# Two attention layers and two graph convolutions on one core: the pair products' place among the source table's tiles, the length of the first burst of pair scatters, and the queue of one small read

## The chip, the cores and the metric

The kernel runs on one core of a Trainium2 chip. A time is the device time of one execution in microseconds (us); the time before is the median of three runs. The engines are TensorE (PE), VectorE (DVE), ScalarE (ACT) and GpSimd (POOL); SyncE (SP) issues transfers only. DMA transfers are issued from SP, ACT or POOL. In this kernel SP and ACT issue the plain ones, and POOL issues the indirect ones, whose row numbers come from a tile of indices.

## What is computed

The graph has N = 1250 nodes and E = 20000 edges, given by `src`, `dst` (sorted by `dst`) and `edge_type_34` (34 relations); a node has D = 768 features. Cut to what matters:

```python
def gatv2(x, src, dst, Ws, bs, Wd, bd, attn):      # attn: H x 768/H
    fs = (x @ Ws + bs).reshape(-1, H, 768 // H)
    fd = (x @ Wd + bd).reshape(-1, H, 768 // H)
    e = leaky_relu(fs[src] + fd[dst], 0.2)
    logits = einsum('ehd,hd->eh', e, attn)
    ex = exp(logits - segment_max(logits, dst)[dst])
    alpha = ex / segment_sum(ex, dst)[dst]
    return elu(segment_sum(alpha[:, :, None] * fs[src], dst))

h = relu(layernorm(x))
g = gatv2(h, W1s, W1d, attn1)                      # 8 heads
g = layer_norm(g + h) * ln1_w + ln1_b
x = x + layer_norm(gatv2(g, Wos, Wod, attno)) * lno_w + lno_b   # 1 head
h = relu(layernorm(x))
# mean of h[src] for each (relation, dst), times W_rel[relation], summed over the relations
h1 = einsum('rni,rio->no', mean, W_rel) + h @ W_root + b_rgcn
out = segment_sum((h1 @ W_gcn)[src] * dinv[src] * dinv[dst], dst) + (h1 @ W_gcn) * dinv**2 + b_gcn
x = x + out
```

Everything is float32.

## The kernel before

**Ranked nodes.** The nodes are ordered by falling degree and cut into ten tiles of 128. Tile k has a fixed number of slots per node, `CAPS = (33, 22, 20, 18, 17, 16, 15, 14, 13, 11)`, 179 in all. Row s of tile k is 128 edges, one for each of its nodes. `fast_front` finds the ranks and writes, with ten indirect scatters on POOL (L938), each node's record into the table `f_rank_d` in DRAM: its number, its degree and its 33 edge slots, 35 int32 (140 bytes). One read (L949) then brings all 1280 records into `rk`, 128 partitions by ten records. From `rk` DVE makes `f_perm` (L950) and `f_permg` (the node numbers), the degrees and the source numbers `rec`; ACT makes `dinv` from the degrees (L1375).

**The source table.** `sources(j)` (L833 to L846) makes 128 rows of the first attention's table f_fs_d: on PE twelve matmuls for the 768 columns and the 8 head sums (L839) and two for the bias (L840), each of which is two instructions in the trace, then two ACT copies into `o_s` (L843, L844), and a write by SP (L845). It is called for tile 0 ahead of the read of the ranked nodes, and for tiles 1 to 9 at the end of `fast_front`. Tile 9 has 98 rows.

**The pair lists.** `pairs()` (L960 to L1088) works out for every edge the place of a record in the table `r_pair_d`, by which the third layer later collects the edges of each (relation, destination) pair. DVE counts the edges of each relation per node and makes three masks; for each mask PE makes a running count over the nodes (L991, L993) and a total (L1000), and ACT copies them out (`pre` L997, `tot` L1002). DVE works on these (from L1007 and L1023), then picks for each of the ten tiles an edge's place out of a table of 34 relations (`pick` L1045, `pl` L1046), and writes `place` (L1088). A small product `fl_ps` (L1083) tells whether the limits on the lists hold.

**The first attention.** `attention` runs over the 179 rows, in chunks of at most 20 rows of one tile (tile 0 in 16 and 17). For each row, `front(c, i)` gathers 128 rows of the source table on POOL (L1164, called with `fs`) into one of 24 buffers, and DVE takes the maximum with the negated destination row (`z`, L1228), multiplies by the attention vector (L1233) and sums by head (L1234). `softmax` (L1240 on) takes a chunk's maximum and has ACT's exp (L1252) and DVE's `den` (L1254). `back(c, i)` scales each row's eight heads on ACT (L1286) and adds it up on PE (L1288), after which the buffer can be gathered into again.

The destination rows of tile k come from `negated1` (L1403 to L1415): a gather of `h` on POOL (L1164), its transposes on PE and copies on ACT (L1123 to L1125), 24 matmul instructions with `f_w1d` (L1135), and `nfd` on DVE (L1414). Program order has this for a tile one or two ahead.

**The pair scatters.** 179 scatters on POOL (L1168, into `r_pair_d`) write the records; each has the `place` of one row of edges as its index. `list_edges(row, slots)` (L1383) adds `slots` to a balance and puts as many scatters as it holds behind the given gather. The first call gives 30, behind the 24th gather of the first attention (L1218); later ones give 0.85 for each gather; 7 and 40 come behind the row scatters of the eighth and ninth tile in `finish1` (L1437), and 4 behind the last gather. What is left of 179 goes by then.

**The order of the work.** The engines run their instructions in order. The program's scheduler settles the order of each engine's instructions from the program's order, the dependences and a plan of times; `issue_after` and manual dependences without a semaphore tell it what is to stand ahead of what. In the kernel before POOL has this order around the change: the rank scatters (L938), the gather of h for tile 0, 24 gathers of source rows, the gathers of h for tiles 1 and 2, 30 pair scatters, then gathers and scatters in turn. PE has the source tiles 1 to 9, the count products, the transposes of tile 0's h, `fl_ps`, the product for tile 0's destination rows, the same for tile 1, and the aggregations. On ACT the copies of tile 1's transposed h stand ahead of the first exp. The weights of the second attention, `wos` and `wod` (SP, L1176) and five rows (ACT, L1181) are loaded into room that `pairs()` gives back.

Of the kernel before, what the change touches and what calls it, by code (L numbers as in the profile page):

```python
# [18 lines left out]
P = 128  # L19
# [6 lines left out]
WIN = 64  # L26

PT = 4
DT = 5
PX = 3  # L30
P2, P3, OC = 160, 32, 6
PC = PT + 3

# [593 lines left out]
def fast_front(ctx, tc, f, x, src, dst, edge_type, W1s, b1s, W1d, b1d, attn1, attno, W_rel):  # L627


    nc = tc.nc  # L630
# [3 lines left out]
    R = W_rel.shape[0]  # L634
# [3 lines left out]
    NT = len(CAPS)  # L638
    NP = NT * P
# [22 lines left out]
    rank_d = dram.tile([NP, 2 + S0], I32, name="f_rank_d")  # L662
# [15 lines left out]
    f.h2_d = dram.tile([NP + P, D], F32, name="r_h2_d")  # L678
    f.ZERO = NP + (PT + 1) * P
    f.h1_d = dram.tile([f.ZERO + 1, D], F32, name="r_h1_d")  # L680
# [3 lines left out]
    with ExitStack() as front:  # L684
# [21 lines left out]
        for j in range(NT):  # L706
            n = min(P, N - j * P)
            t = xp.tile([P, D], F32, name=f"x{j}", tag=f"x{j}")
            nc.sync.dma_start(t[:n], x[j * P:j * P + n, :])
            xs.append(t)  # L710
        QW = HW + H // 2
        w1s = wp.tile([P, KC, 2, QW], F32, name="w1s")
# [72 lines left out]
        hT = early.tile([P, KC, NP], F32, name="hT")  # L785
        for j in range(NT):
            n = min(P, N - j * P)
            row = xs[j]
            sc, sh = norm_scale(nc, small, f, row, n)
            nc.scalar.activation(row[:n], row[:n], AF.Relu, bias=sh[:n], scale=sc[:n])  # L790
            nc.sync.dma_start(f.h0_d[j * P:j * P + n, :], row[:n])
            to_columns(nc, ps_t, f, hT, j, row, n, both=True)
        xstack.close()

# [4 lines left out]
        fill = prep.tile([P, COLS, 3], I32, name="fill")  # L799
# [3 lines left out]
        nc.vector.tensor_scalar(fill[:, :, 0], ones_c, lane, None, op0=ALU.mult)  # L803
        for t in range(PT + 1):
            cols = fill[:, :R * PC, 1].rearrange("p (r c) -> p r c", c=PC)[:, :, t] if t < PT else fill[:, R * PC:, 1]
            n = R if t < PT else PX
            nc.vector.tensor_scalar(cols, ones_c[:, :n], lane, float(t * P), op0=ALU.mult, op1=ALU.add)
        nc.vector.memset(fill[:, :R * PC, 1].rearrange("p (r c) -> p r c", c=PC)[:, :, PT:], 0)
        nc.sync.dma_start(f.pair_d.rearrange("(p c) f -> p c f", p=P), fill)
        zero = prep.tile([P, D], F32, name="zero")  # L810
        nc.vector.memset(zero, 0.0)
        nc.sync.dma_start(f.h2_d[NP:, :], zero)
        for t in range(PT + 1):
            nc.sync.dma_start(f.h1_d[NP + t * P:NP + (t + 1) * P, :], zero)
        nc.sync.dma_start(f.h1_d[f.ZERO:, :], zero[:1])


        quarter = SLOPE / (1.0 - SLOPE)
# [14 lines left out]
        def sources(j):  # L833

            n = min(P, N - j * P)
            ps = ps_m.tile([P, 2, 512], F32, name="ps", tag="ag")
            for half in range(2):
                for k in range(KC):
                    nc.tensor.matmul(ps[:n, half, :QW], hT[:, k, j * P:j * P + n], w1s[:, k, half], start=(k == 0), stop=False)  # L839
                last = nc.tensor.matmul(ps[:n, half, :QW], ones_row[:, :n], bias1[:, half], start=False, stop=True)  # L840
            o = work.tile([P, H, HD + 1], F32, name="o_s", tag="o_s", bufs=3)
            ov = o.rearrange("p (a h) d -> p a h d", a=2)
            nc.scalar.copy(ov[:n, :, :, :HD], ps[:n, :, :HW].rearrange("p a (h d) -> p a h d", d=HD))  # L843
            nc.scalar.copy(ov[:n, :, :, HD], ps[:n, :, HW:QW])  # L844
            nc.sync.dma_start(f.fs_d[j * P:j * P + n, :], o[:n].rearrange("p h e -> p (h e)"))  # L845
            return last  # L846

        gotf = prep.tile([P, NT, RW], F32, name="gotf")
        nc.vector.tensor_copy(gotf, got)
# [49 lines left out]
        for g in range(2):  # L899
            wide = ps_m.tile([P, 2, 512], F32, name="wide", tag="ag").rearrange("p a b -> p (a b)")  # L900
            for lo, hi in ((0, 512), (512, N // 2)):
                at = slice(g * (N // 2) + lo, g * (N // 2) + hi)
                nc.tensor.matmul(wide[:, lo:hi], ones16[:EP], flat2[:, at], start=True, stop=False)
                last = nc.tensor.matmul(wide[:, lo:hi], big16[:EP], flat[:, at], start=False, stop=True)
# [39 lines left out]
        with tc.issue_after(last_keys.ins):  # L944
            sources(0)


        rk = prep.tile([P, NT, 2 + S0], I32, name="rk")
        nc.sync.dma_start(rk, rank_d.rearrange("(k p) f -> p k f", p=P))  # L949
        nc.vector.tensor_copy(f.perm, rk[:, :, 0])  # L950
        nc.vector.tensor_scalar(f.permg, rk[:, :, 0], float(N - 1), None, op0=ALU.min)
        nc.vector.tensor_copy(f.degf, rk[:, :, 1])
# [7 lines left out]
        def pairs():  # L960
            tri = pp.tile([P, P], BF16, name="tri")
            nc.vector.tensor_scalar(tri, iota_f, iota_p, 1.0, op0=ALU.subtract, op1=ALU.is_gt)
            ones_b = pp.tile([P, P], BF16, name="ones_b")
# [21 lines left out]
            mask = pp.tile([P, 3, NT, R], BF16, name="mask")  # L985
            pre, tot = [], []
            for i in range(3):
                nc.vector.tensor_scalar(mask[:, i], cnt, float(i + 1), None, op0=ALU.is_ge)
                pps = ps_t.tile([P, 2, 512], F32, name="pp", tag="mm2")
                ppv = pps[:, 0, :NT * R].rearrange("p (k r) -> p k r", r=R)  # L990
                nc.tensor.matmul(ppv, tri, mask[:, i], start=True, stop=False)  # L991
                for k in range(NT - 1):
                    nc.tensor.matmul(ppv[:, k + 1:, :], ones_b,  # L993
                                     mask[:, i, k:k + 1, :].to_broadcast([P, NT - 1 - k, R]),
                                     start=False, stop=(k == NT - 2))
                a = pp.tile([P, NT, R], F32, name=f"pre{i}")
                nc.scalar.copy(a, ppv)  # L997
                tp = pps[:, 1, :]
                for k in range(NT):
                    nc.tensor.matmul(tp[:, :R], ones_b, mask[:, i, k, :], start=(k == 0), stop=(k == NT - 1))  # L1000
                b = pp.tile([P, R], F32, name=f"tot{i}")
                nc.scalar.copy(b, tp[:, :R])  # L1002
                pre.append(a)
                tot.append(b)

            for i in range(2):
                nc.vector.tensor_sub(pre[i], pre[i], pre[i + 1])  # L1007
# [35 lines left out]
            for k, S in enumerate(CAPS):  # L1043
                t = pp.tile([P, R, S0], F32, name="pick", tag="pick")
# [7 lines left out]
            later = pp.tile([P, NT, S0], F32, name="later")  # L1052
# [34 lines left out]
            nc.vector.tensor_scalar(pad, pad, none, None, op0=ALU.add)  # L1087
            nc.vector.scalar_tensor_tensor(f.place, pad, float(P * COLS), pl, op0=ALU.mult, op1=ALU.add)  # L1088

        for j in range(1, NT):  # L1090
            sources(j)
        rows_only.close()
        ranking.close()
        pp = front.enter_context(tc.tile_pool(name="f_pp", bufs=1, side="right"))
# [50 lines left out]
def fast_rest(ctx, tc, f, x, src, dst, edge_type, W1s, b1s, W1d, b1d, attn1, ln1_w, ln1_b,  # L1145
              Wos, bos, Wod, bod, attno, lno_w, lno_b, W_rel, W_root, b_rgcn, W_gcn, b_gcn, out):
    nc = tc.nc
    N, D, NT, NP, KC, HW, S0 = f.N, f.D, f.NT, f.NP, f.KC, f.HW, f.S0
    R = W_rel.shape[0]
# [39 lines left out]
    def attention(H, table, negated, attn_e, first, loads, finish, rate, rest, give_back=lambda: None):  # L1189
# [21 lines left out]
        def front(c, i):  # L1211

            t, s = c.t, c.first + i
            fs = pool.tile([P, RW], F32, name="fs", tag="fs", bufs=ring)
            row = gather(fs[:, :W], table[:, :], f.rec[:, t.k, s, 0:1])
            fs = fs[:, :W].rearrange("p (h e) -> p h e", h=H)
            if t.k == 0 and s == ring - 1:
                list_edges(row, 30)  # L1218
            elif t.k or s >= ring:
                list_edges(row, rate)  # L1220
            if t.k == NT - 1 and s == t.S - 1:
                list_edges(row, rest)
                f.last_row = row
            if t.lg is None:
                lg = pool.tile([P, S0 * f.H], F32, name="lg", tag="lg", bufs=2)
                t.lg = lg[:, :S0 * H].rearrange("p (s h) -> p s h", h=H)
            z = rows_tile("z", 2)
            nc.vector.tensor_tensor(z, fs, t.nfd, op=ALU.max)  # L1228
            if H == 1:
                nc.vector.scalar_tensor_tensor(z[:, 0, :], z[:, 0, :], 1.0, attn_e[:, 0, :], op0=ALU.mult,  # L1230
                                               op1=ALU.mult, accum_out=t.lg[:, s, :])
            else:
                nc.vector.tensor_mul(z, z, attn_e)  # L1233
                nc.vector.tensor_reduce(t.lg[:, s, :], z, axis=AX.X, op=ALU.add)  # L1234
            c.rows.append(fs)
# [81 lines left out]
        for k, S in enumerate(CAPS):  # L1317
            parts = -(-S // CHUNK)
            assert parts <= 2
            for i in range(parts):  # L1320
                c = Tile()
                c.k, c.first, c.n, c.rows = k, S * i // parts, S * (i + 1) // parts - S * i // parts, []
                chunks.append(c)
        tiles = {}
# [58 lines left out]
    def list_edges(row, slots):  # L1383

        due[0] += slots
        while due[0] >= 1.0:
            due[0] -= 1.0
            if edges:
                k, s = edges.pop(0)
                with tc.issue_after(row.ins):  # L1390
                    scatter(pair_d[:, :], f.rec[:, k, s, :], f.place[:, k, s:s + 1], "pair",
                            bounds_check=P * COLS - 1, oob_is_err=False)
# [207 lines left out]
    ahead = first_half(0)  # L1600
# [14 lines left out]
    nc.vector.tensor_copy(own_f, f.perm)  # L1615
    adj = rq.tile([P, NT, DT * P], F32, name="adj")
    srcz = rq.tile([P, NT, S0], I32, name="srcz")
# [19 lines left out]
    wgcn = rq.tile([P, KC, D], F32, name="wgcn")  # L1637
    slots_left = [(k, s) for k in range(DT) for s in range(CAPS[k])]

    slots_each = len(slots_left) / (2 * R)  # L1640
    with three:
        adjacency_slots(ahead)
        for i in range(len(jobs)):
# [3 lines left out]
            ahead = first_half(i + 1) if i + 1 < len(jobs) else None  # L1647
# [9 lines left out]
    with ExitStack() as four:  # L1657
# [32 lines left out]
        def by_rows(k):  # L1690

            acc = gp.tile([P, D], F32, name="acc", tag="acc", bufs=NT - DT)
            gather(acc, h1_d[:, :], f.permg[:, k:k + 1])
# [19 lines left out]
        neighbours(0, 4 * P)  # L1713
        neighbours(4 * P, DT * P)
        for k in range(NT - 1, DT - 1, -1):
            by_rows(k)
            if NT - 1 - k < DT:
                last(NT - 1 - k)
# [48 lines left out]
```

## Time and profile before

| | us |
|---|---|
| median of three runs | 2768.38 |
| lowest and highest run | 2763.95, 2773.92 |
| the profiled execution | 2772.99 |
| its span | 2771.2 |
| busy PE / DVE / POOL / ACT in the span | 2355.7 / 1560.9 / 1549.0 / 852.4 |

The mean granted TensorE clock was 0.930. By stretches of the span (busy us of each engine; POOL's busy time leaves out about 0.3 us between two of its transfers):

| stretch | what runs | PE | DVE | ACT | POOL |
|---|---|---|---|---|---|
| 112 to 175 | source tiles 1 to 9, count products begin | 62.15 | 32.83 | 5.88 | 0.00 |
| 175 to 257 | pair places, first rows of the first attention | 26.77 | 80.01 | 4.76 | 62.73 |
| 257 to 292 | first aggregation, pair scatters | 29.77 | 15.79 | 34.09 | 28.44 |
| 292 to 400 | first attention, steady | 63.09 | 98.20 | 73.18 | 88.07 |

A line of a timeline reads: start in the span and duration in us, engine, line of the kernel, operation, the tile written and the tiles read, shapes, how many instructions are folded into the line, and in brackets how long the engine had been idle before it and what ended the wait. L1164 and L1168 are two helpers, for all gathers and all scatters, so those are told apart by the names of their tiles.

### The profile page before, as it was taken

What the parts mean: (1) busy time and instruction counts of PE and PEld (TensorE: products, weight loads), DVE (VectorE), ACT (ScalarE), POOL (GpSimd) and SP (SyncE); (2) the same over time, 40 slices, a digit from 0 to 9 for tenths busy, and PEclk for the clock granted to TensorE, in tenths of its full rate; (3) what the DMA queues carried; (4) which work ended last, traced back from release to release, by engine and by line L of the source; (5) the groups of instructions that cost most, each with busy time, mean ns of one, the idle gap of its engine ahead of it and who ended that gap; (6) DMA issues with size and microseconds to landing.
All of it is one profiled execution on the core that took longest, in us unless ns stands there. A gap on an engine that the chain in (4) does not pass through costs nothing. (4 is left out here: it accounts for less than half of the span.)

```text
span 2771.2 us, 24164 instructions
## 1 busy us (share of the span) xinstructions
PE 2355.7 (85%) x7759; PEld 1365.4 (49%) x7759; DVE 1560.9 (56%) x2360; ACT 852.4 (31%) x2308; POOL 1549.0 (56%) x1113
## 2 busy tenths in 40 slices
PE   3874484889998467889899999999999999999687
PEld 2431142445545234444456666666666666666254
DVE  7659779999996799999563222222232222210262
ACT  3003592778773122333312112211221212212010
POOL 3137787777872675778375544444444454431471
PEclk7986797999999788999999999999999999999899
DMA  7134453444540775677477777777777777766783
GB/s 248 41 128 146 115 147 95 127 129 131 154 123 29 246 234 170 202 214 216 160 241 194 200 189 187 189 197 197 192 194 187 185 191 197 174 165 152 217 264 117
DMA packets 136419, 476.82 MB, mean 172 GB/s; under 512 B 26323, under 2 KB 28396, under 8 KB 136285
## 3 DMA queue, kind: packets, MB, share of 16 engines
q0 software_dynamic: 83872, 334.60, 46.4%
q1 hardware_dynamic: 47755, 134.03, 13.6%
q10 hardware_dynamic: 4658, 6.57, 0.7%
q8 instruction: 64, 1.05, 0.1%
q14 instruction: 70, 0.57, 0.1%
HBM read 385.90 MB, written 89.32 MB: 171 GB/s over the span
## 5 line engine op out<-in xcount | busy, mean ns | idle before, releaser
L1135 PE MATMUL ps<-wrel,mT 128*128 128x384 f32 x3336 | 1099.1, 486 | 1.1 <-DMA wrel<-in_L_gnn_W_rel_dram 1.1
L1135 PEld LDWEIGHTS ps<-wrel,mT 128*128 128x128 f32 x3336 | 623.0, 190 | 407.1 <-DMA wrel<-in_L_gnn_W_rel_dram 1.0
L1164 POOL DMA_INDIRECT g<-r_h_d,lists x241 | 341.9, 1419 | 516.9 <-DVE g L1565 290.7
L1288 PE MATMUL ag<-fs,identf 128*128 128x384 f32 x716 | 286.9, 532 | 152.4 <-ACT fs L1286 142.0
L1565 DVE TENSOR_TENSOR g<-g,g 128x768 f32<-128x768 f32 x68 | 64.6, 950 | 612.5 <-DMA g<-r_h_d,lists 512.6
L1228 DVE TENSOR_TENSOR z<-fs,nfd 128x776 f32<-128x776 f32 (+1 forms) x358 | 348.5, 990 | 60.0 <-DMA fs<-f_fs_d,rec 37.2
L1286 ACT ACTIVATE fs<-fs,lg 128x96 f32<-128x96 f32 x1376 | 370.0, 363 | 0.3
L1278 PE MATMUL ag<-fs,dg 128*128 128x384 f32 x716 | 251.7, 512 | 81.0 <-ACT dg L1276 81.0
L1168 POOL DMA_INDIRECT r_pair_d<-rec,place x179 | 259.5, 1450 | 59.9 <-issue 46.7
L1164 POOL DMA_INDIRECT fs<-r_fs_d,rec x179 | 244.0, 1363 | 80.7 <-issue 33.4
L1592 POOL DMA_INDIRECT r_h_d<-y,lists x139 | 223.9, 1611 | 110.2 <-ACT y L1591 52.3
L1164 POOL DMA_INDIRECT fs<-f_fs_d,rec x179 | 236.7, 1323 | 77.0 <-issue 50.2
L1288 PEld LDWEIGHTS ag<-fs,identf 128*128 128x128 f32 x716 | 132.4, 200 | 294.0 <-ACT fs L1286 236.5
L1278 PEld LDWEIGHTS ag<-fs,dg 128*128 128x128 f32 x716 | 141.3, 200 | 188.0 <-ACT dg L1276 88.1
L1591 ACT ACTIVATE y<-ps,lists 128x768 f32<-128x768 f32 x71 | 64.0, 901 | 479.8 <-PE ps L1135 479.8
L1591 ACT ACTIVATE y<-ps,rcnt 128x768 f32<-128x768 f32 x68 | 61.3, 901 | 454.6 <-PE ps L1135 454.6
L1230 DVE SCALAR_TENSOR_TENSOR z<-z,attn_o 128x769 f32<-128x769 f32 x179 | 174.4, 993 | 0.0
L1697 DVE TENSOR_TENSOR acc<-acc,nb 128x768 f32<-128x768 f32 x69 | 66.2, 959 | 187.1 <-DMA nb<-r_h_d,srcz 186.3
L1233 DVE TENSOR_TENSOR z<-z,attn 128x776 f32<-128x776 f32 x179 | 168.5, 955 | 0.1
L1234 DVE TENSOR_REDUCE lg<-z 128x8 f32<-128x776 f32 x179 | 168.0, 950 | 0.1
L1627 DVE SCALAR_TENSOR_TENSOR arow<-node,from_f,arow 128x1250 f16<-128x1250 f16 x110 | 166.2, 1511 | 1.7
L1123 PEld LDWEIGHTS pt<-identf,g 128*128 128x128 f32 x834 | 99.8, 141 | 47.5 <-issue 24.5
(282 smaller groups left out, 2322.0 us busy)
## 6 DMA issues: line engine op xcount, KB each, us to landing
wrel<-in_L_gnn_W_rel_dram SPq DMA_DIRECT2D x37, 2304.0 KB
g<-r_h_d,lists POOLq DMA_INDIRECT x241, 4.8
r_nfd_d<-fd SPq DMA_DIRECT2D x10, 384.0 KB
nfd<-r_nfd_d SPq DMA_DIRECT2D x10, 384.0 KB
r_x_d<-xb SPq DMA_DIRECT2D x10, 384.0 KB
x1r<-r_x_d SPq DMA_DIRECT2D x10, 384.0 KB
f_fs_d<-o_s SPq DMA_DIRECT2D x9, 388.0 KB
x<-in_x_dram SPq DMA_DIRECT2D x9, 384.0 KB
```

Source lines behind the costliest of these rows:

```text
L1135: last = nc.tensor.matmul(ps[:n, half, :f.HW], hT[:, k, j * P:j * P + n], w[:, k, cols], start=(k == 0), stop=(k == f.KC - 1 and not bias))
L1164: return nc.gpsimd.indirect_dma_start(out=to, out_offset=None, in_=table, in_offset=bass.IndirectOffsetOnAxis(ap=idx, axis=0))
L1168: s = nc.gpsimd.indirect_dma_start(out=table, out_offset=bass.IndirectOffsetOnAxis(ap=idx, axis=0), in_=rows, in_offset=None, **kw)
L1228: nc.vector.tensor_tensor(z, fs, t.nfd, op=ALU.max)
L1230: nc.vector.scalar_tensor_tensor(z[:, 0, :], z[:, 0, :], 1.0, attn_e[:, 0, :], op0=ALU.mult, op1=ALU.mult, accum_out=t.lg[:, s, :])
L1233: nc.vector.tensor_mul(z, z, attn_e)
L1234: nc.vector.tensor_reduce(t.lg[:, s, :], z, axis=AX.X, op=ALU.add)
L1278: nc.tensor.matmul(c.ps[:, half, :HW], dg, fs[:, 0, half * HW:(half + 1) * HW], start=begin, stop=end)
L1286: nc.scalar.activation(fs[:, h, :HD], fs[:, h, :HD], AF.Copy, scale=t.lg[:, s, h:h + 1])
L1288: nc.tensor.matmul(c.ps[:, half, :HW].rearrange("p (h d) -> p h d", d=HD), f.identf, fs[:, half * H // 2:(half + 1) * H // 2, :HD], start= ...
L1592: s = nc.gpsimd.indirect_dma_start(out=h1_d[:, :], out_offset=bass.IndirectOffsetOnAxis(ap=j.node, axis=0), in_=y, in_offset=None, compute ...
L1627: nc.vector.scalar_tensor_tensor(a, node16, from_f[:, k, s:s + 1], a, op0=ALU.is_equal, op1=ALU.add)
```

## The change

The ranked nodes are read by POOL instead of SP. The tenth source tile's twelve matmuls and its last bias product get a dependence, without a semaphore, on the last of the count products, so that they stand behind them on PE. The first burst of pair scatters is 24 instead of 30. The zero writes of four tables are told to stand behind the last write of `h0`.

```diff
+TL = 9
...
-            nc.sync.dma_start(f.h0_d[j * P:j * P + n, :], row[:n])
+            h0_write = nc.sync.dma_start(f.h0_d[j * P:j * P + n, :], row[:n])
...
-        nc.sync.dma_start(f.pair_d.rearrange("(p c) f -> p c f", p=P), fill)
+        with tc.issue_after(h0_write.ins):
+            nc.sync.dma_start(f.pair_d.rearrange("(p c) f -> p c f", p=P), fill)
...
         def sources(j):
 
             n = min(P, N - j * P)
+            mine = []
...
-                    nc.tensor.matmul(ps[:n, half, :QW], hT[:, k, j * P:j * P + n], w1s[:, k, half], start=(k == 0), stop=False)
+                    mine.append(nc.tensor.matmul(ps[:n, half, :QW], hT[:, k, j * P:j * P + n], w1s[:, k, half],
+                                                 start=(k == 0), stop=False))
                 last = nc.tensor.matmul(ps[:n, half, :QW], ones_row[:, :n], bias1[:, half], start=False, stop=True)
+            mine.append(last)
...
-            return last
+            return mine
...
-        nc.sync.dma_start(rk, rank_d.rearrange("(k p) f -> p k f", p=P))
+        nc.gpsimd.dma_start(rk, rank_d.rearrange("(k p) f -> p k f", p=P))
...
-                    nc.tensor.matmul(tp[:, :R], ones_b, mask[:, i, k, :], start=(k == 0), stop=(k == NT - 1))
+                    ahead = nc.tensor.matmul(tp[:, :R], ones_b, mask[:, i, k, :], start=(k == 0), stop=(k == NT - 1))
...
+            for i in behind:
+                tc.add_manual_dep(i.ins, ahead.ins.name, mybir.DependencyInfo(
+                    mybir.DependencyClass.NoSync, mybir.DependencyReason.DATA), reason="the table's last tiles later")
...
-        for j in range(1, NT):
+        for j in range(1, TL):
             sources(j)
+        behind = []
+        for j in range(TL, NT):
+            behind += sources(j)
...
-                list_edges(row, 30)
+                list_edges(row, 24)
```

The writes of zeros to `h2_d` and `h1_d` get `issue_after` like that of `pair_d`; on SP they stood behind the `h0` writes already.

How the order of the instructions moves, engine by engine: on PE the three passes of count products stand between the ninth and the tenth source tile, and ACT's copies follow. On SP the read of the ranked nodes is gone (it stood behind two writes of `o_s` and ahead of eight). On POOL that read stands behind the rank scatters, ahead of tile 0's gather of h; then come 24 gathers, 24 pair scatters, the gathers of h for tiles 1 and 2, and gathers and scatters in turn; before the tenth tile's row scatter there are 13 pair scatters instead of 7. On DVE all of the picks up to `place` stand ahead of the first `nfd` and the first `z`, where the first seven or so rows' z instructions stood between them.

More of the change, by code (lines that the diff above doesn't have):

```diff
@@ L808, in fast_front @@
         nc.vector.memset(fill[:, :R * PC, 1].rearrange("p (r c) -> p r c", c=PC)[:, :, PT:], 0)
-        nc.sync.dma_start(f.pair_d.rearrange("(p c) f -> p c f", p=P), fill)
+        with tc.issue_after(h0_write.ins):
+            nc.sync.dma_start(f.pair_d.rearrange("(p c) f -> p c f", p=P), fill)
         zero = prep.tile([P, D], F32, name="zero")
         nc.vector.memset(zero, 0.0)
-        nc.sync.dma_start(f.h2_d[NP:, :], zero)
+        with tc.issue_after(h0_write.ins):
+            nc.sync.dma_start(f.h2_d[NP:, :], zero)
         for t in range(PT + 1):
-            nc.sync.dma_start(f.h1_d[NP + t * P:NP + (t + 1) * P, :], zero)
-        nc.sync.dma_start(f.h1_d[f.ZERO:, :], zero[:1])
+            with tc.issue_after(h0_write.ins):
+                nc.sync.dma_start(f.h1_d[NP + t * P:NP + (t + 1) * P, :], zero)
+        with tc.issue_after(h0_write.ins):
+            nc.sync.dma_start(f.h1_d[f.ZERO:, :], zero[:1])
         quarter = SLOPE / (1.0 - SLOPE)
```

## Prediction

> **What bounds the kernel now.** I read the times first. The profiled execution took 2772.99 us and its span is 2771.2 us. The median of the three runs is 2768.38 us, 4.6 us less. I work on the clock of the profiled span and put the shift that comes out onto the median. About 0.3%, 8.3 us, is what a measurement of this kernel can tell from no change.
>
> Second I read the page's busy shares: PE 85%, DVE 56%, POOL 56%. They are averages over stages. The change sits between 106 us and 290 us, so I next read each engine's timeline there. This is the source table's last tile and what follows it, from the timeline of PE:
>
> ```profile
> 162.56 4.15 PE L839 MATMUL ps<-w1s,hT 128*98 128x388 f32 x12
> ...
> 172.37 0.32 PE L991 MATMUL pp<-mask,tri 128*128 128x340 bf16 x1
> ...
> 179.06 0.44 PE L1000 MATMUL pp<-mask,ones_b 128*128 128x34 bf16 x10 [0.53 <-ACT pre L997]
> ```
>
> The tenth tile holds PE from 162.56 to 172.4 (9.8 us), and then the three passes of count products run to 179.5 (7.1 us). DVE waits for the products, from its timeline:
>
> ```profile
> 174.60 0.18 DVE L1023 TENSOR_SCALAR more<-tot 128x34 f32<-128x34 f32 x1 [29.31 <-ACT tot L1002]
> ...
> 187.04 1.33 DVE L1045 TENSOR_TENSOR pick<-same,pdf 128x1122 f32<-128x1122 f16 x1
> ...
> 195.67 0.96 DVE L1414 SCALAR_TENSOR_TENSOR nfd<-ps,bias 128x768 f32<-128x768 f32 x1 [0.29 <-PE ps L1135]
> ...
> 225.69 0.49 DVE L1088 SCALAR_TENSOR_TENSOR place<-pad,pl 128x330 int32<-128x330 f32 x1
> ...
> 291.02 0.97 DVE L1228 TENSOR_TENSOR z<-fs,nfd 128x776 f32<-128x776 f32 x1 [19.21 <-DMA fs<-f_fs_d,rec]
> ```
>
> DVE is idle for 29.3 us ahead of 174.60, then without a gap to 271.8, and then idle for 19.2 us until the 25th source row is there. That row is late because of POOL, from its timeline:
>
> ```profile
> 177.15 1.16 POOL L1164 DMA_INDIRECT h<-f_h_d,f_permg  x1 [71.91 <-DVE hit L1062]
> ...
> 217.42 1.49 POOL L1164 DMA_INDIRECT h<-f_h_d,f_permg  x1 [0.30 <-issue]
> ...
> 226.47 2.37 POOL L1168 DMA_INDIRECT r_pair_d<-rec,place  x1 [5.54 <-DVE place L1088]
> ...
> 272.96 0.97 POOL L1168 DMA_INDIRECT r_pair_d<-rec,place  x1 [0.30 <-issue]
> ...
> 287.00 0.99 POOL L1164 DMA_INDIRECT fs<-f_fs_d,rec  x1 [0.30 <-PE ag L1288]
> ```
>
> The 30 pair scatters hold POOL from 226.47 to 286.7. Under an unbroken stream of z rows one scatter passes every 2.62 us, the length of one row's three DVE instructions; with DVE idle one takes 0.97 plus 0.30 (1.28 us). The 25th gather stands behind them. After 292 POOL sets the pace: in 292 to 400 it has 65 instructions, 88.07 us busy, and 65 gaps of 0.30 fill 107.6 of the 108 us. So the number to follow is **when the 25th gather issues, now 287.00**: a shift of it goes through to the end.
>
> **The change part by part.**
>
> *Ranked nodes by GpSimd's queue.* SP now issues the read at 106.89 (0.37 us) and DVE uses it at 109.68, 2.79 us later. PE's next tile waits for it too, since ACT, in its order, has dinv (which needs the ranked nodes) ahead of the table's copies: PE stands idle 9.86 us until 111.15. So a delay d here moves all that follows. Nothing is queued on POOL behind it until the h gather at 177, and the SP writes that stood behind it lose nothing. The trace has no POOL transfer of this shape (1280 runs of 140 bytes). Bounds: d is 0 if it costs what SP's does. The upper end takes the shortest 128-row gather, 0.94 us, as if all of it were by row: 7.4 ns for each of 1280 rows, 9.4 us, d = +9. Between: the shortest 32-row gathers (g at L1164) take 0.86 us and the shortest 128-row one 0.94, so about 0.8 ns a row over a fixed 0.84: 1.9 us for 1280 rows, and with some 2.4 us of landing 4.3 us, d = **+1.5**. I take that, as it separates the fixed part.
>
> The Trainium skill, "DMA: Bandwidth & Descriptors", Specifications, speaks against this step: first byte at about 1 us by the gpsimd path, about 0.6 us by the sync path. By that alone d would be an estimated +0.4; no run here shows such a read on POOL yet.
>
> *Products ahead of the tenth tile.* On PE the products move 9.8 us earlier (162.6 + d), the tenth tile 7.1 us later (to 179.5 + d). ACT's copies go along. DVE starts its chain at 164.8 and the first pick 12.4 us later at 177.2. Today 39.06 us lie between the first pick and the end of the place at 226.1; 19 z instructions at 0.875 (16.6), one nfd (0.87) and 0.3 of idle are in it, so the picks alone take 21.3 us. The changed program has all of them ahead of nfd and the z's: **place at 198.5 + d instead of 226.1**.
>
> *What is late next.* The h gather of tile 0 waits for every write of the table to land, the tenth tile's too: now 4.7 us after PE ends it (172.4 to 177.15), so at 184.2 + d, 7.1 us later. From gather to nfd is 18.5 us now, of which 1.3 are PE waiting for the flag's product, gone afterwards: nfd at 201.5 + d, against 195.67. DVE is idle for 3 us there, which costs nothing yet, since DVE has 19.2 us of waiting to give.
>
> *The order on POOL.* First burst 24, not 30. But the scatters now stand behind the 24th gather and **ahead of the h gathers of tiles 1 and 2**; today those go first. ACT, in order, has the copies of tile 1's columns ahead of the first exp, and PE has that tile's transposes and product ahead of the first aggregation. So tile 1's h gather, which now issues at 217.42 with time to spare, gets onto the path: from its issue 4.1 us to the transposes (as at 177.15 to 181.26), 1.5 for them, 9.7 for the product, 1.1 for row 0's aggregation: **25th gather at h + 16.4**. Break-even is h at 270.6.
>
> When does h issue (without d)? POOL starts the gathers at 185.7. Today's 24 take 38.5 us, 1.6 each. By 202.4, when z starts, 10.4 have gone. The other 13.6 go under z rows: at 1.6 they end at 224.2, at 2.62 at 238.0. From nfd DVE has 0.87, then 55 z instructions at 0.875 and 1.2 of small ones until it must wait for the exp, at 251; until then scatters pass at 2.62, that is 10.2 of them or 5. The other 13.8 or 19 pass beside an idle DVE at 1.28: h at 268.7 or 275.3. Middle 272, with d 273.5; 25th gather at 289.9: **+2.9 us**. DVE agrees: exp some 8.2 us after h (transposes, copies, table), then den and 12.6 us of rows left, 25th z at h + 21.6 = 295.1 against 291.02, +4.1, of which a few gathers that have gone ahead by then give some back. ACT starts its 128 scalings (34.1 us) some 25 us later, but its next exp (322.93) has 31.8 us of slack now.
>
> *Weights.* The wos and wod loads (2304 KB each) wait for the place and come at 198.5 instead of 226, beside the gathers. The windows there show 243 to 294 GB/s; the rows are used at one per 2.62 us and have 16 us of lead, so I cost it at nothing. Without that cover POOL's gathers get later; that is in the 2.62 bound.
>
> *The six scatters less* go to the burst between the last two row scatters of the first attention, 7 to 13. Those 7 run from 882.59 to 892.2, 1.37 each; 13 end near 900, and the next row scatter waits for DVE until 905.36: hidden, 5 us to spare. The new issue orders of the zero writes move nothing.
>
> Which price holds for POOL under z's? At 226 to 254 the pitch is 2.62; at 292 to 400, with DVE busy 98.2 of 108 us, it is 1.65. The Trainium skill, "SBUF — State Buffer", Who interferes with whom, says that a DVE instruction with two SBUF inputs shuts out a GpSimd one that reads SBUF, and that a reduce doesn't. The first stretch agrees, the second only in part. By the rule each costs a z row: h at 275.3, an estimate of +6.2 in all.
>
> **The rivals.**
>
> *About the same (forecast):* +2.9, 2768.4 + 2.9 = **2771**. Speaks for it: both ends of the POOL sum lie within 5 us of break-even.
>
> *Faster:* POOL passes its DMAs at 1.65 under z's, as at 292 to 400. Gathers end at 224, 16.2 scatters pass by 251, the other 7.8 take 10: h at 261, 25th gather 277.4 + d. With d = 0, -9.6, **2759**. Against it: one scatter per 2.62 us in the very stretch of z's that this one repeats. At 1.28 throughout DVE would set the 25th z near 267 and the time near 2745, which no stretch under z's shows.
>
> *Slower, the other side:* the h gather of tile 1 behind 24 scatters becomes the bound. If gathers go at 2.62 and the remaining 19 scatters at their mean of 1.45 + 0.30 even while DVE waits, h is at 284.3, with d 285.8, 25th gather 302.2: +15, **2784**. It decides from h later than 270.6. For it: nothing else can release ACT and PE. Against: beside an idle DVE each takes 1.28.
>
> *The read costs by row on POOL:* d = +9 instead of 1.5, **2779**.
>
> *It does nothing:* the picks come early but nothing waits for them, and h lands at break-even: 2768.
>
> **How the numbers follow.** Forecast and nothing together 0.56; faster 0.17; slower through the h gather 0.19; slower through the read 0.08. The range goes from a little under the faster case to a little short of the slow one: 2757 to 2782.
>
> **What would show it.** The first product on PE near 164, the place near 200, the h gather of tile 0 near 186, nfd near 203. The read's use on DVE 4.3 us after its issue. On POOL, 24 scatters between the 24th gather and tile 1's h, that one near 273; DVE's idle time ahead of den, about 30 us from 252, in place of the 19.2 at 291; 25th gather near 290. I am wrong if h issues before 262 or after 279, if the read takes over 8 us, or if ACT's late scalings hold up row 25 to 32.

## The result and the profile after

The changed kernel takes 2780.74 us (median of 7 runs, 2776.43 to 2791.15); the kernel before, with four more runs, 2773.01. The ratio is 1.0045, with a 95% interval of 1.0029 to 1.0061: slower by 8 to 17 us. The profiled execution took 2778.47 us, with a span of 2776.7.

Around the change it went nearly as the forecast had it. The timeline of PE after:

```profile
162.95 0.32 PE L999 MATMUL pp<-mask,tri 128*128 128x340 bf16 x1
...
168.90 0.40 PE L1008 MATMUL pp<-mask,ones_b 128*128 128x34 bf16 x10 [0.53 <-ACT pre L1005]
169.15 4.13 PE L845 MATMUL ps<-w1s,hT 128*98 128x388 f32 x12
```

The products start 9.4 us earlier, and the tenth tile follows them. The timeline of DVE after:

```profile
110.50 0.17 DVE L958 COPY f_perm<-rk 128x10 int32<-128x10 int32 x1 [20.37 <-DMA rk<-f_rank_d]
...
176.35 1.33 DVE L1056 TENSOR_TENSOR pick<-same,pdf 128x1122 f32<-128x1122 f16 x1
...
199.90 0.50 DVE L1099 SCALAR_TENSOR_TENSOR place<-pad,pl 128x330 int32<-128x330 f32 x1
200.32 0.95 DVE L1428 SCALAR_TENSOR_TENSOR nfd<-ps,bias 128x768 f32<-128x768 f32 x1
...
278.58 0.38 DVE L1268 TENSOR_REDUCE den<-lg 128x8 f32<-128x128 f32 x1 [28.36 <-ACT lg L1266]
```

The place is ready at 200.4 instead of 226.2, and the 19.2 us that DVE waited for the 25th row are gone. In their place DVE waits 28.4 us, from 250.2 on, for ACT's first exp, ahead of den. The timeline of POOL after:

```profile
106.90 1.03 POOL L957 DMA_DIRECT2D rk<-f_rank_d  x1 [1.91 <-DMA f_rank_d<-rec,rank_i]
183.80 1.03 POOL L1178 DMA_INDIRECT h<-f_h_d,f_permg  x1 [75.88 <-DVE pick L1056]
...
228.25 3.77 POOL L1182 DMA_INDIRECT r_pair_d<-rec,place  x1 [0.30 <-issue]
...
270.92 0.99 POOL L1178 DMA_INDIRECT h<-f_h_d,f_permg  x1 [0.30 <-issue]
272.22 0.96 POOL L1178 DMA_INDIRECT h<-f_h_d,f_permg  x1 [0.30 <-issue]
287.13 2.27 POOL L1178 DMA_INDIRECT fs<-f_fs_d,rec  x1 [13.94 <-PE ag L1302]
```

The scatters come right behind the gathers (228.25), tile 1's h gather stands behind all 24 at 270.92, and POOL waits 13.94 us for the first aggregation. The 25th gather issues at 287.13, against 287.00 before. So up to here the change has neither won nor lost, and the question is what costs the 8 to 17 us after that.

### The profile page after: what moved, and what is told of

Its sections match the earlier page's. It is cut to its first block, busy times and chain, and to the rows that moved or that the text cites. A ratio compares the mean times of both kernels' runs of the same rounds, so it can differ in the third digit from the quotient of the medians.

```text
span 2776.7 us, 24171 instructions
## 1 busy us (share of the span) xinstructions
PE 2347.5 (85%) x7759; PEld 1364.6 (49%) x7759; DVE 1562.6 (56%) x2360; ACT 852.0 (31%) x2308; POOL 1536.9 (55%) x1114
## 5 line engine op out<-in xcount | busy, mean ns | idle before, releaser
L1302 PE MATMUL ag<-fs,identf 128*128 128x384 f32 x716 | 279.1, 522 | 111.6 <-ACT fs L1300 101.3
L1178 POOL DMA_INDIRECT fs<-f_fs_d,rec x179 | 243.6, 1361 | 94.0 <-issue 49.7
L1182 POOL DMA_INDIRECT r_pair_d<-rec,place x179 | 253.2, 1414 | 56.4 <-issue 46.0
L1711 DVE TENSOR_TENSOR acc<-acc,nb 128x768 f32<-128x768 f32 x69 | 66.2, 959 | 184.2 <-DMA nb<-r_h_d,srcz 183.5
L1137 PE MATMUL pt<-identf,h 128*128 128x128 f32 x120 | 22.1, 334 | 123.0 <-DMA h<-f_h_d,f_permg 82.5
```

The costliest lines, as they stand in the source:

```text
L1178: return nc.gpsimd.indirect_dma_start(out=to, out_offset=None, in_=table, in_offset=bass.IndirectOffsetOnAxis(ap=idx, axis=0))
L1182: s = nc.gpsimd.indirect_dma_start(out=table, out_offset=bass.IndirectOffsetOnAxis(ap=idx, axis=0), in_=rows, in_offset=None, **kw)
L1302: nc.tensor.matmul(c.ps[:, half, :HW].rearrange("p (h d) -> p h d", d=HD), f.identf, fs[:, half * H // 2:(half + 1) * H // 2, :HD], start= ...
```

## The experiments

Each run is compared with the kernel before on the same chip, in five rounds. In the table the shift of the 25th gather is against 287.00, from one profile each; the time in us is the ratio less one, times 2770.

| run | 25th gather | ratio (95%) | us |
|---|---|---|---|
| **read by SP or ACT, or another small read on POOL** | | | |
| products, burst 30 | +6.0 | 1.0031 (1.0019 to 1.0044) | +8.6 |
| products, burst 24 | -1.1 | 1.0017 (1.0007 to 1.0026) | +4.7 |
| burst 24 | -6.2 | 0.9971 (0.9957 to 0.9986) | -8.0 |
| burst 24, read by ACT | -6.0 | 0.9968 (0.9955 to 0.9980) | -8.9 |
| burst 24, five memsets on POOL | -7.5 | 0.9975 (0.9964 to 0.9986) | -6.9 |
| burst 24, and one record read on POOL | -6.8 | 0.9978 (0.9965 to 0.9991) | -6.1 |
| burst 24, and 640 records read on POOL | -5.2 | 0.9977 (0.9964 to 0.9989) | -6.4 |
| products, burst 24, h gather first | -7.9 | 0.9971 (0.9959 to 0.9983) | -8.0 |
| products, burst 20, h gather first | -10.6 | 0.9956 (0.9941 to 0.9971) | -12.2 |
| burst 20 | -14.4 | 0.9952 (0.9935 to 0.9968) | -13.3 |
| **1280 records read on POOL** | | | |
| the read alone (burst 30) | +2.4 | 1.0015 (1.0003 to 1.0027) | +4.2 |
| the whole change | +0.1 | 1.0045 (1.0029 to 1.0061) | +12.5 |
| the whole change, h gather first | -8.8 | 1.0008 (0.9995 to 1.0022) | +2.2 |
| burst 24 and the read | -7.9 | 1.0007 (0.9996 to 1.0018) | +1.9 |
| burst 24, second read that nobody uses | -6.9 | 1.0001 (0.9990 to 1.0013) | +0.3 |
| burst 24, the read, sixteen memsets | -8.4 | 1.0001 (0.9990 to 1.0012) | +0.3 |
| burst 25 and the read | -5.7 | 0.9987 (0.9976 to 0.9997) | -3.6 |
| burst 20 and the read | -13.0 | 0.9942 (0.9926 to 0.9957) | -16.1 |

**The parts alone.** The read:

```diff
-        nc.sync.dma_start(rk, rank_d.rearrange("(k p) f -> p k f", p=P))
+        nc.gpsimd.dma_start(rk, rank_d.rearrange("(k p) f -> p k f", p=P))
```

> The kernel before with one edit: the ranked nodes are read by GpSimd's queue. The profile after shows 3.60 us from issue to use against 2.79, so by the theory of the forecast (what comes later at the 25th gather comes later at the end) this is +0.8 us, no change to be seen. By the rival that the read carries the loss (its queue, or what it does to the transfers behind it), this alone is +8 us or more.

Measured +4.2 us (0.8 to 7.5): more than the 0.8, less than the 8. Undecided by itself. The burst:

```diff
-                list_edges(row, 30)
+                list_edges(row, 24)
```

> The kernel before with one edit: a first burst of 24 pair scatters instead of 30. By the theory that the 25th gather sets the end, POOL has 6 scatters of 1.28 us less ahead of it: the 25th gather at 279.3 instead of 287.0 and a time 6 to 8 us lower. By the rival that the six scatters cost as much where they go (the burst behind the ninth tile's row scatter, or between gathers), the time is as before or higher by up to 8 us.

Measured -8.0 us, the 25th gather at 280.77. DVE's wait for the 25th row has shrunk by 7.7 us, which is six scatters of 1.28; timeline of DVE with the burst of 24 alone:

```profile
284.70 0.97 DVE L1228 TENSOR_TENSOR z<-fs,nfd 128x776 f32<-128x776 f32 x1 [11.47 <-DMA fs<-f_fs_d,rec]
```

So the burst is a gain by itself, and the scatters that it drops cost nothing where they go. The products alone, which is the changed kernel with

```diff
-        nc.gpsimd.dma_start(rk, rank_d.rearrange("(k p) f -> p k f", p=P))
+        nc.sync.dma_start(rk, rank_d.rearrange("(k p) f -> p k f", p=P))
...
-                list_edges(row, 24)
+                list_edges(row, 30)
```

> The changed kernel with the read on SP's queue again and the burst of 30: the move of the count products alone. By the theory that the 25th gather sets the end, the h gather of tile 1 stands behind six scatters more, 270.9 - 0.8 + 6 x 1.28 = 277.8, and the 25th gather comes at 294: +7 us against before, and 7 us over the run with the burst of 24. By the rival that the loss of the change arises behind the 25th gather, from ACT's scalings that start 22 us late, this run loses about as much as the one with the burst of 24 and the two lie within 3 us.

and with the first of these two edits only:

> The changed kernel with the read on SP's queue again; the count products ahead of the tenth tile and the burst of 24 stay. By the theory of the forecast it lies 0.8 us under the changed kernel, and by its 25th gather at 286.3 no more than 1 us from before. By the rival that the read carries the loss it is as before or faster. By the rival that the loss arises behind the 25th gather from ACT's late scalings it is 8 to 12 us over before, as the changed kernel is.

The products alone are +8.6 us, with tile 1's h gather at 276.30 and the 25th gather at 293.02, within 2 us of what was expected. With the burst of 24 it is +4.7 us where the 25th gather promised -1.1: an excess of 5.8, for which its interval leaves 3 to 8. The whole change lies another 7.8 us higher, and all it has more is the read.

**Is it the h gather's place?** Tile 1 is begun two rows earlier, so that its h gather is ahead of the 24th gather:

```diff
-                if i == now.n // 2:
+                if i == (6 if j == 0 and H > 1 else now.n // 2):
                     begin(j + 2)
```

> The changed kernel with tile 1's h gather ahead of the 24th gather (the tile is begun two rows earlier), so that exp and the aggregations don't wait for the 24 scatters. The theory that the h gather's place behind the scatters costs time: exp near 250, DVE streams on to 266, scatters at one per 2.62 us until then and at 1.28 after, the 25th gather near 280 instead of 287 and a time 6 to 8 us under the changed kernel. The rival that the loss lies elsewhere (the read, or ACT's and PE's backlog behind the 25th gather for another reason): within 2 us of the changed kernel.

> As the run before it, with the ranked nodes read by SP's queue again: the products ahead of the tenth tile, the burst of 24 and tile 1's h gather ahead of it. If the read costs what its own span shows, it lies 0.8 us under that run; if the read costs what the runs of the first group showed, 2 to 8 us under it. By the 25th gather's place it lies 6 to 8 us under before, about where the burst of 24 alone lies: the products' move is then worth nothing even without its side effect.

Both are 10 to 13 us under the same kernels without the edit, and their 25th gathers 7 to 9 us earlier: the h gather behind the scatters is what made the products' move lose. With SP's read the excess of 5.8 is gone as well (gather -7.9, time -8.0). But the two differ by 0.37%, some 10 us, in nothing but the read. And -8.0 us is just what the burst alone gives, so the products' move itself has gained nothing.

**The read on another base, and how far the burst goes.** The read's edit and the burst of 24 on the kernel before; then the kernel before with `list_edges(row, 20)`:

> The kernel before with a burst of 24 and the read on GpSimd's queue; products and h gathers stay. By the read's own span (3.6 us from issue to use, not 2.79) it is 0.8 us over the run with the burst of 24 alone, 2763. By the rival that the read costs more than its span, it is 4 us or more over it, 2766 to 2770.

> The kernel before with a burst of 20 alone. By the theory of the 25th gather, ten scatters less are 12.8 us less ahead of it: it issues near 274 and DVE's wait of 19.2 us is down to about 6. The ten go to the burst between the last two row scatters: 17 at 1.37 are 23.3 us of the 24 there, just hidden. So 9 to 13 us under before, 2 to 5 under the burst of 24. By the rival that the tail's burst is already full with 13 (margin 5 us), it is no faster than the burst of 24.

The read costs 0.36% again, 10 us. The burst of 20 is the fastest kernel so far, 2755.56 us: DVE's wait is down to 6.51 us, and the 17 scatters just fit. Timelines of DVE and of POOL with the burst of 20:

```profile
276.67 0.97 DVE L1228 TENSOR_TENSOR z<-fs,nfd 128x776 f32<-128x776 f32 x1 [6.51 <-DMA fs<-f_fs_d,rec]
```

```profile
867.05 0.98 POOL L1168 DMA_INDIRECT r_pair_d<-rec,place  x1 [0.30 <-issue]
...
888.46 0.97 POOL L1168 DMA_INDIRECT r_pair_d<-rec,place  x1 [0.30 <-issue]
890.29 0.96 POOL L1168 DMA_INDIRECT r_fs_d<-fs,f_perm  x1 [0.86 <-DVE wt L1433]
```

The row scatter of the tenth tile now waits only 0.86 us for DVE, where 13.16 us were free before: nothing is left there for a still shorter burst.

**What of the read costs 10 us?** The profiles with the burst of 24 and the 1280 records on POOL have one thing in common that their twins lack: POOL stands still for 2.2 us ahead of its 280th transfer (without the read it is the 279th), and the trace shows nothing that it would wait for. Timeline of POOL with the burst of 24 alone, then with the read too:

```profile
644.12 0.96 POOL L1164 DMA_INDIRECT fs<-f_fs_d,rec  x1 [7.87 <-issue]
645.39 1.01 POOL L1168 DMA_INDIRECT r_pair_d<-rec,place  x1 [0.31 <-issue]
```

```profile
641.97 0.96 POOL L1164 DMA_INDIRECT fs<-f_fs_d,rec  x1 [6.79 <-issue]
645.12 1.00 POOL L1168 DMA_INDIRECT r_pair_d<-rec,place  x1 [2.18 <-PE ag L1288]
```

(A wait on PE is what the profile puts down to it; this scatter waits in the program only for an earlier transfer of its own queue.) Four runs, each on the kernel before with the burst of 24: five tiny instructions on POOL, without the read; a second read beside SP's; the read with sixteen instructions; the read on ACT's queue:

```diff
-        shift = prep.tile([P, P], F32, name="shift")
+        shift, idle = prep.tile([P, P], F32, name="shift"), prep.tile([P, 1], F32, name="idle"); [nc.gpsimd.memset(idle, 0.0) for _ in range(5)]
```

> The kernel before with a burst of 24, the read on SP's queue, and five tiny memsets more on POOL early on, while it is idle; no other instruction moves. In the three runs with the read on POOL and a burst of 24, POOL stands still for 2.2 us ahead of its 280th transfer (near 645) beside a load of program code, and in their twins with the read on SP it doesn't. If that stall comes of where POOL's code lies, five instructions more can bring it up here too, with 2770 to 2773. If it comes of one transfer more in POOL's queue, or of the read's own lateness, this run stays at the burst of 24, 2762 to 2765, without the stall.

```diff
+        rk2 = prep.tile([P, NT, 2 + S0], I32, name="rk2"); nc.gpsimd.dma_start(rk2, rank_d.rearrange("(k p) f -> p k f", p=P))
```

> The kernel before with a burst of 24, the read on SP's queue as before, and a second read of the same records on POOL's queue into a tile that nobody uses. If the loss comes of one transfer more in POOL's queue (its count, its descriptors) or of the code that it adds, this run shows the 2.2 us stall near 645 and 2770 to 2773. If it comes of the ranked nodes' being used 0.8 us later, it stays at 2762 to 2765.

> The kernel before with a burst of 24 and the read on POOL, and sixteen tiny memsets more on POOL early on. If the loss comes of where POOL's code lies, the stall ahead of the 280th transfer goes or moves and the time falls from 2773 towards 2764. If it comes of the transfer's place in the queue, both stay: the stall at the 280th transfer and 2770 to 2774.

```diff
-        nc.sync.dma_start(rk, rank_d.rearrange("(k p) f -> p k f", p=P))
+        nc.scalar.dma_start(rk, rank_d.rearrange("(k p) f -> p k f", p=P))
```

> The kernel before with a burst of 24 and the read on ACT's queue; POOL's program is that of the burst of 24. If the loss of the read comes of POOL's program or queue, this run has no stall near 645 and stays within 2 us of the burst of 24, 2762 to 2766. If any move of the read off SP loses (a later use, another order of SP's writes), it lies at 2768 or more.

The second read, which nobody uses, costs as much as the real one within the noise (1.0001 against 1.0007), with the ranked nodes coming by SP on time; and it has the stall. So the loss is not the lateness of what is read. The read on ACT's queue loses nothing, and five instructions more on POOL lose nothing and bring no stall: the loss comes with the read's being on POOL. Sixteen instructions beside the read change nothing either. The runs with five and with sixteen instructions don't settle whether it matters where POOL's code lies: in both, the load of program code that the profile records (at 646.0 and 640.1) stands beside the same transfer as without the memsets.

Is it one transfer more, or what it moves? A second read of a single record (`rank_d[:1, :]`), and of 640:

> The kernel before with a burst of 24, the read on SP's queue, and a read of one single record on POOL's queue that nobody uses. If one transfer more in POOL's queue makes the loss, whatever it moves, POOL stands still for 2.2 us ahead of its 280th transfer and the time is 2770. If the number of records makes it, there is no such stall and the time stays at 2762 to 2764.

> The same with a read of 640 records on POOL's queue that nobody uses. If the number of records moves the stall to another transfer of POOL, it is not ahead of the 280th, or is gone, and the time lies between 2762 and 2770. If the count of transfers makes it, the stall is ahead of the 280th and the time is 2770.

These ran on a chip where the kernel before took 2778.13, so only ratios count. Both keep most of the burst's gain and neither has the stall: a transfer more is not it, and half the records is not it. Nor is it the length of POOL's program alone: the page counts 1114 instructions on POOL in both, as with the second read of 1280.

> The products ahead of the tenth tile, the read on SP's queue, tile 1's h gather ahead of the burst, and a burst of 20. If the move of the products is worth nothing once the 25th gather is freed by a shorter burst, this lies within 3 us of the burst of 20 alone, 2755.6. If the earlier places do help then, it is 4 us or more below it.

The products' move adds nothing to the burst of 20 (0.9956 against 0.9952).

At last, the read with bursts of 25 and of 20:

> The kernel before with the read on POOL's queue and a burst of 25. If the loss belongs to the place in POOL's queue, the 280th transfer is another one here, the stall is not at the same pair scatter, or is gone, and the time is the burst of 24's plus one scatter, a ratio near 0.998. If the loss belongs to the read, wherever the queue stands, the ratio is 1.000 to 1.001 as with the burst of 24.

> The kernel before with the read on POOL's queue and a burst of 20. If the loss belongs to the read in general, the ratio is 0.3% over that of the burst of 20 (0.9952), 0.998 to 0.999. If it belongs to the place in the queue, it is 0.995 to 0.997.

With the burst of 20 the read costs nothing (0.9942 against 0.9952), and no stall is there. With 25 the 280th transfer is a gather; POOL waits 9.36 us ahead of it, where the kernels with the burst of 24 wait 6.7 to 7.9 at that gather, so some 2 us of a stall may be in it. The ratio, 0.9987, lies between the two expectations. So the loss does not belong to the read in general. It comes with 1280 records more on POOL and certain places of what follows, and what stops POOL there the traces don't show.

**Where the time goes.** A wait that all kernels that lose by the read have in common comes later, at the last gather of h, for the tenth tile. PE's transposes (`pt`) wait for it, and they do so too with the read alone and the burst of 30, where no stall stands ahead of the 280th transfer. Timeline of PE with the products, the burst of 24 and SP's read, then with the whole change:

```profile
792.81 0.82 PE L1137 MATMUL pt<-identf,h 128*128 128x128 f32 x6
```

```profile
799.88 1.51 PE L1137 MATMUL pt<-identf,h 128*128 128x128 f32 x6 [7.04 <-DMA h<-f_h_d,f_permg]
```

PE then comes late with the next destination rows, and DVE falls back between its rows 159 and 173. The table has the pairs without and with the 1280 records on POOL, in us. Wait and rows are from one profile each; the last column is the difference of the two ratios, times 2770.

| pair | PE's wait, without and with | rows 159 to 173 longer by | time |
|---|---|---|---|
| products, burst 24 | 0.00, 7.04 | 8.3 | 7.8 |
| products, burst 24, h gather first | 0.85, 7.04 | 8.7 | 10.2 |
| burst 24 | 0.77, 6.97 | 8.5 | 10.0 |
| burst 24, memsets (5 and 16) | 0.00, 3.47 | 6.4 | 7.2 |
| burst 24, second read | 0.77, 2.96 | 3.4 | 8.3 |
| burst 30 (the kernel before, and the read alone) | 0.78, 3.42 | 5.3 | 4.2 |
| burst 20 | 0.00, 0.00 | 1.0 | -2.8 |

In the thirteen other kernels (without the 1280 records on POOL, or with them and a burst of 20 or 25) PE waits 0.85 us at most. So this wait goes with the read's price, and but for the second read it is nearly as large. No run moves this gather alone, so it is not shown that the wait makes the loss.

## Why the prediction was right or wrong

*The products and the place:* right. First product 162.95 (forecast 162.6 + d), first pick 176.35 (177.2 + d), place 200.40 (198.5 + d).

*What is late next:* right, to within 3 us. Tile 0's h gather at 183.80 (184.2 + d), nfd at 200.32 (201.5 + d).

*POOL behind the products:* right, inside its bounds. The gathers end at 227.95, between 224.2 and 238.0; DVE stops at 250.2 (251); h issues at 270.92 (268.7 to 275.3, plus d), and the 25th gather 16.2 us later (16.4). The forecast of +2.9 at this point was too high by 2.8, mostly as h came at 270.92 and not at 273.5.

*Which price under z's:* the pitch of 2.62 us held. DVE streams here in pairs of rows, and POOL passes two transfers per pair: timeline of POOL after, under the z rows.

```profile
212.51 3.69 POOL L1178 DMA_INDIRECT fs<-f_fs_d,rec  x1 [0.30 <-issue]
216.51 0.95 POOL L1178 DMA_INDIRECT fs<-f_fs_d,rec  x1 [0.30 <-issue]
217.76 3.69 POOL L1178 DMA_INDIRECT fs<-f_fs_d,rec  x1 [0.30 <-issue]
221.75 0.95 POOL L1178 DMA_INDIRECT fs<-f_fs_d,rec  x1 [0.30 <-issue]
```

Timeline of DVE beside it:

```profile
211.80 1.83 DVE L1242 TENSOR_TENSOR z<-fs,nfd 128x776 f32<-128x776 f32 x2
213.55 1.83 DVE L1247 TENSOR_TENSOR z<-z,attn 128x776 f32<-128x776 f32 x2
215.30 1.82 DVE L1248 TENSOR_REDUCE lg<-z 128x8 f32<-128x776 f32 x2
```

From one long transfer to the next are some 5.24 us, twice 2.62. The Trainium skill, "SBUF — State Buffer", Who interferes with whom, says that a DVE instruction with two SBUF inputs keeps out a GpSimd one that reads SBUF and a reduce doesn't; the alternation of 3.69 and 0.95 agrees with that where DVE streams without a gap.

*A shift of the 25th gather goes through to the end:* it held in the times, for the burst and for the products. Over the ten runs without the 1280 records on POOL, gather shifts from -14.4 to +6.0 gave times from -13.3 to +8.6, each within 3 us but one. Row by row the shift is not carried so evenly: in the profile with the burst of 24 alone DVE's 25th row is 6.3 us earlier than before, its 179th 1.8, and the end 7.7. The one is the products with the burst of 24, where the time is 5.8 us above the gather. The forecast priced ACT's late start (tile 1's copies behind the scatters) at nothing, as its next exp had 31.8 us of slack. With h first, so ACT not late, the excess is gone, so this price may have been too low, by 3 to 8 us in that run. But with the products and the burst of 30, where h comes 7.7 us later still (276.30), the excess is only 2.6, and its interval leaves -1 to +6. That ACT's late start is the cause is not shown, and through which wait the excess comes was not found.

*The read:* **this is the step that failed.** The forecast had d = +1.5 as lateness of the ranked nodes, between 0 and 9. The lateness is +0.8: 3.60 us from issue to use against 2.79, 1.03 us of them on POOL. (The Trainium skill, "DMA: Bandwidth & Descriptors", Specifications, with 1 us against 0.6 for the first byte, pointed to +0.4; the trace shows twice that.) But the read costs 7.8 us in the whole change (1.0045 against 1.0017), 10 in two other pairs, and 8.3 when nobody uses what it reads. The forecast looked for what stood behind the read on POOL, found tile 0's h gather some 70 us later, and let the term end there. What came lies further down that engine: the stall 545 us behind the read, and 688 us behind it the last gather of h (794.87), for which PE waits 7.04 us where it waits for nothing with SP's read. The rival of a price by row gave +10.4 in sum (2779), near what came, but its mechanism, a slow read, did not happen: 1.03 us on POOL, not 9.4.

*The sum:* the products +8.6, the burst of 24 behind them -3.9 (1.0017 against 1.0031), the read +7.8: +12.5, against +2.9 forecast. Of the difference of 9.6, 6.3 is the read. The rest, 3.3, belongs to the products with the burst of 24 (+4.7 against +1.4 forecast): the excess of 5.8 less the 2.5 by which their 25th gather came earlier than forecast. It is little more than the interval of that run, 2.7 either way.

*The slower rival,* h behind 24 scatters at 284.3, did not come: they passed at 1.28 beside an idle DVE.

What stays open: what holds POOL at its 280th transfer, and what makes the last gather of h late. The stall is only a part of that. From the 280th transfer (652.18) to that gather POOL takes 142.7 us in the whole change; with SP's read, from the 279th (649.34), it takes 137.9.

## What to carry to other kernels

In an in-order queue, work that becomes ready earlier is put ahead of something: look at what it displaces. Here earlier scatters pushed one h gather back, and that gather held ACT, PE and DVE. Where a queue sets the pace, the cheapest gain was to move part of its burst to a place where it idles: ten scatters of 1.28 us gave 13 us, until 17 filled the 23 us there. And when an edit moves a transfer to another queue, price the queue as well as the transfer: a dummy transfer that nobody uses tells the two apart in one run.

## What the runs showed that was not expected

POOL issues a plain read of 1280 records of 140 bytes in 1.03 us, hardly more than an indirect gather of 128 rows (0.94). Its time on POOL grows little with the records: 0.59 us for one, 0.93 for 640. That read, with 1280 records but not with 640 or with 1, came with a stop of 2.2 us ahead of POOL's 280th transfer, 534 to 545 us later, in all five profiles with the burst of 24 (the change among them), and in none with 20 or 30. And in all six profiles with it and a burst of 24 or 30, PE waited 3 to 7 us for the last gather of h.
